# A conditional residual adapter on Trainium2: the opening puts the rows into four partition quarters with one product, shuffles 17 of them, and copies W1 later

## The chip, the cores and the metric

The kernel runs on one core of a Trainium2 chip. The metric is the device time of one execution in microseconds. Several engines work side by side, each in the order of its own queue: PE (TensorE, matrix products), DVE (VectorE), ACT (ScalarE), POOL (GpSimd), and SP (SyncE), which here only issues transfers (DMAs).

## The reference

There are 128 batches of a 128 x 512 activation. Each batch has a language id; the id selects one of ten sets of weights.

```python
w1 = W1[language_ids]                      # 512 x 128 for each batch
w2 = W2[language_ids]                      # 128 x 512
h = relu(einsum('bsh,bha->bsa', x, w1) + b1[language_ids][:, None, :])
adapted = einsum('bsa,bah->bsh', h, w2) + b2[language_ids][:, None, :]
y = x + adapted
normed = (y - mean(y)) * rsqrt(var(y) + 1e-5)          # over the 512
out = x + normed * gamma[language_ids][:, None, :] + beta[language_ids][:, None, :]
```

All data are float32. gamma, beta, b1 and b2 are drawn, so none of them can be left out.

## The kernel before

**One batch.** The 128 sequence positions lie on the partitions. PE transposes x in four 128 x 128 pieces into PSUM (`transpose_x`, L235), ACT copies them to SBUF (`copy_xT`, L239), PE makes four products with the batch's W1 (`down`, L258), ACT applies the relu with b1 as bias (`relu`, L266), and PE makes the product with W2 (`up`, L275) into one of five PSUM buffers called py. DVE adds x and sums the row (`residual`, L292), ACT squares and sums (`square`, L315), small operations make the mean and the reciprocal deviation, DVE subtracts the mean and multiplies with gamma (`scale`, L358), then multiplies with the deviation and adds (`finish`, L367). What is added there was made earlier by POOL: o = x + beta (`add_beta`, L252). b2 is added in one of three ways: by POOL as r = x + b2 (`add_b2`, L245), by DVE in PSUM (`vector_b2`, L285), or by PE as a second product into the same PSUM buffer (`b2_by_matmul`, L274). A py buffer is free again when `finish` has read it, so `up(b)` waits for `finish(b-5)`.

**The loop.** Iteration i issues on PE `transpose_x(i)`, `down(i-1)` and `up(i-2)`; the vector work of batch i-3 follows. All orders on the engines are written out by hand: `keep` chains each instruction to the one before it on its engine.

**The tables.** beta, gamma and b2 are ten rows of 512 each, and every engine needs the row of its batch on all 128 partitions. So an opening spreads all 30 rows: the rows are split into three bf16 parts (`parts`, 96 partitions), and for each row a product with a 0/1 column of `pick` puts the sum of the three parts on all 128 partitions (`spread`, L206), from where DVE or ACT copies it to its table (L211, L209). The 30 rows are interleaved with the work of the first four batches. Before that PE makes products of ones that nobody reads (`spin`, L486).

**The weights.** W2 is kept whole in SBUF. W1 comes three ways. Batches 0 to 8 load their own W1 from HBM (`load_first`, L154). From batch 9 on ACT copies it from a table in SBUF (`stage_w1`, L226): batches 9 to 20 (`EARLY = 21`) from w1e, whose rows are laid out so that the transposes of x must take every fourth column; later ones from w1, loaded in four pieces of 640 KB (`load_w1`, L103) in iterations 8, 10, 12 and 14, with transposes of adjacent columns. SP issues in this order: ids, gamma, x of batches 0-1, W2 of three languages, W1 of batches 0 and 1, x 2-3, W1 2 and 3, the rest of W2, x 4-5, W1 4 and 5, x 6-7, W1 6 and 7, x 8-9, half of w1e, W1 8, the other half of w1e, x 10-11, then x 12-15 and on in fours. The small rows of beta, b2 and b1 come by ACT's queue.

**The end.** The last five batches have an order of their own (`tail`), in which POOL takes part of the last multiplications and additions.

Of the kernel before, what the change touches and what calls it, by code (L numbers as in the profile page):

```python
# [16 lines left out]
P = 128  # L17
G = 4
EPS = 1e-5
FIRST = 9  # L20
EARLY = 21
LATE = 12
U = 2

# [2 lines left out]
def cond_resid_kernel(ctx: ExitStack, tc: tile.TileContext, x, itok, W1, b1, W2, b2, gamma, beta, out):  # L27
# [18 lines left out]
    def keep(ins):  # L46

        engine = ins.ins.engine
        if engine in last:
            tc.add_manual_dep(ins.ins, last[engine], behind, reason="kept order")  # L50
        last[engine] = ins.ins.name
        return ins
# [31 lines left out]
    x_0 = xp.tile([P, G, H], FP, tag="x", name="x_0")  # L84
    xs[0] = x_0

    def load_part(lo, hi):
        dst = xs[lo // G][:, lo % G : lo % G + hi - lo, :]
        keep(nc.sync.dma_start(out=dst, in_=x[lo:hi].rearrange("b s h -> s b h")))

    keep(nc.sync.dma_start(out=ids, in_=itok.rearrange("(o b) -> o b", o=1)))
    keep(nc.scalar.dma_start(out=rows[0:L, :], in_=beta))
# [1 line left out]
    keep(nc.scalar.dma_start(out=rows[2 * L : 3 * L, :], in_=b2))  # L94
    load_part(0, 2)
    keep(nc.scalar.dma_start(out=b1r, in_=b1))

    warm = const.tile([P, 1], FP, name="warm")
    keep(nc.vector.memset(warm, 1.0))
    keep(nc.scalar.activation(warm, warm, AF.Abs_reciprocal_sqrt))  # L100
    def load_w1(k):
        keep(
            nc.sync.dma_start(out=w1[:, :, k, :], in_=W1[:, k * P : (k + 1) * P, :].rearrange("l p a -> p l a"))  # L103
        )

    ident = const.tile([P, P], FP, name="ident")
    make_identity(nc, ident)
    eps = const.tile([P, 1], FP, name="eps")
    nc.gpsimd.memset(eps, EPS)
    ones = const.tile([P, P], BF, name="ones")  # L110
    nc.gpsimd.memset(ones, 1.0)

    R = 3 * L
    parts = const.tile([P, H], BF, name="parts")
    keep(nc.vector.memset(parts.bitcast(mybir.dt.uint32), 0))
    pick = const.tile([96, R], BF, name="pick")
    both = st.tile([P, R], FP, tag="both", name="both", bufs=1)[:96, :]
    keep(nc.vector.tensor_tensor(both, ident[:96, 0:R], ident[:96, 32 : 32 + R], ALU.add))  # L120
    keep(nc.vector.tensor_tensor(pick, both, ident[:96, 64 : 64 + R], ALU.add))
    keep(nc.vector.tensor_scalar(pick[:, L : 2 * L], pick[:, L : 2 * L], -0.5, None, ALU.mult))

    lids, w1s = {}, {}

# [25 lines left out]
    def load_first(b):  # L151
        w1s[b] = wp.tile([P, KC, A], FP, tag="w1s", name=f"w1s_{b}")
        src = W1[bass.ds(lid(b, ET.SP), 1)].rearrange("o (p k) a -> p (o k a)", k=KC)
        keep(nc.sync.dma_start(out=w1s[b].rearrange("p k a -> p (k a)"), in_=src))  # L154
# [9 lines left out]
    load_w2(0, 3)  # L164
    load_first(0)
    load_first(1)
    load_part(2, G)
    load_first(2)
    load_first(3)
    load_w2(3, L)  # L170
    xs[1] = xp.tile([P, G, H], FP, tag="x", name="x_1")
    for b in (G, G + 2):
        load_part(b, b + 2)
        load_first(b)
        load_first(b + 1)
    xs[2] = xp.tile([P, G, H], FP, tag="x", name="x_2")
    load_part(2 * G, 2 * G + 2)
    load_early(0, 5)
    load_first(2 * G)
    load_early(5, L)  # L180
    load_part(2 * G + 2, 3 * G)

    left = rp.tile([P, H], FP, tag="r", name="left")
    keep(nc.vector.tensor_copy(parts[0:R, :], rows[0:R, :]))
    keep(nc.vector.tensor_tensor(left[32 : 32 + R, :], rows[0:R, :], parts[0:R, :], ALU.subtract))
    keep(nc.vector.tensor_copy(parts[32 : 32 + R, :], left[32 : 32 + R, :]))
    keep(nc.vector.tensor_tensor(left[64 : 64 + R, :], left[32 : 32 + R, :], parts[32 : 32 + R, :], ALU.subtract))
    keep(nc.vector.tensor_copy(parts[64 : 64 + R, :], left[64 : 64 + R, :]))

    b1T = const.tile([P, L], FP, name="b1T")  # L190

# [10 lines left out]
    def spread(r, copier):  # L202
        t = (beta_b, gamma_b, b2_b)[r // L]
        row = p_y.tile([P, H], FP, tag="y", name=f"row_{r}")
        pick_r = pick[:, r : r + 1].to_broadcast([96, P])
        keep(nc.tensor.matmul(row, lhsT=pick_r, rhs=parts[:96, :], start=True, stop=True))  # L206
        dst = t[:, r % L * H : (r % L + 1) * H]
        if copier is nc.scalar:
            keep(nc.scalar.copy(dst, row))  # L209
        else:  # L210
            keep(nc.vector.tensor_copy(dst, row))  # L211

    xT, hT, rs, os, ys, ssqs, nmeans, rstds = {}, {}, {}, {}, {}, {}, {}, {}
    phs, pxs, sums = {}, {}, {}


    def b2_by_matmul(b):
        return b in (5, B - 2, B - 1)

    def b2_by_vector(b):  # L220
        return b < 4 or 8 <= b < B - 8 and (b % 4 == 1 if b < 24 else b % 16 in (1, 6, 11) or b % 32 == 30)

    def stage_w1(b):
        w1s[b] = wp.tile([P, KC, A], FP, tag="w1s", name=f"w1s_{b}")
# [43 lines left out]
    def up(b):  # L268
        v = lid(b, ET.PE)
        ys[b] = p_y.tile([P, H], FP, tag="y", name=f"py_{b}")  # L270
        m = b2_by_matmul(b)
        if m:
            pick_b = pick[:, bass.ds(v + 2 * L, 1)].to_broadcast([96, P])
            keep(nc.tensor.matmul(ys[b], lhsT=pick_b, rhs=parts[:96, :], start=True, stop=False))  # L274
        keep(nc.tensor.matmul(ys[b], lhsT=hT[b], rhs=w2[:, bass.ds(v * H, H)], start=not m, stop=True))  # L275
        del hT[b]
# [27 lines left out]
    def scalar_means(g):  # L304
        nmeans[g] = st.tile([P, 2], FP, tag="nmean", name=f"nmean_{g}")
        keep(nc.scalar.activation(nmeans[g], sums[g], AF.Copy, scale=-1.0 / H))  # L306
# [36 lines left out]
    def deviation(g):  # L343
        root(ssqs[g], of_pair(g)[0])
# [29 lines left out]
    def on(b):  # L374
        return 0 <= b < B
# [106 lines left out]
    def spin(n, width):  # L482
        idle = p_s.tile([P, H], FP, tag="s", name="idle")
        for _ in range(n):
            keep(
                nc.tensor.matmul(  # L486
                    idle[:, :width], lhsT=ones, rhs=ones[:, 0:1].to_broadcast([P, width]), start=True, stop=True
                )
            )


    spin(9, H)
    spin(1, H // 2)

    def spread_turn(lo, hi):
        for r in range(lo, hi):
            spread(r, nc.scalar if r % 7 in (1, 3, 5) else nc.vector)

    def x_turn(b):
        transpose_x(b)  # L500
        copy_xT(b)

    x_turn(0)
    transpose_b1()
    spread_turn(0, 4)
    x_turn(1)
    spread_turn(4, 11)
    down(0)
    relu(0)
    spread_turn(11, 15)  # L510
    down(1)
    relu(1)
    x_turn(2)
    spread_turn(15, 19)
    x_turn(3)
    down(2)
    relu(2)
    spread_turn(19, 24)
    down(3)
    relu(3)  # L520
    spread_turn(24, R)
    up(0)
    up(1)

    for i in range(3, B + U):
        b = i - U - 1
        if b > G and b % G == 2 and b // G + 3 < NG:
            load_x(b // G + 3)
        if i == 5:
            load_x(3)  # L530
        if i in (8, 10, 12, 14):
            load_w1((i - 8) // 2)
        if i == 4:
            up(2)
        if i == 5:
            up(3)
        if i > 3 and on(i):
            transpose_x(i)
        if b <= E:
            add_b2(b + 2)  # L540
            add_beta(b)
        if i > 4 and on(i - 1):
            down(i - 1)
        if i > 3 and on(i):
            copy_xT(i)
        if b == 2:
            scalar_means(0)
            deviation(0)
        if i > 4 and on(i - 1):
            relu(i - 1)  # L550
        if i + 1 >= LATE and on(i + 1):
            stage_w1(i + 1)
        if i > 5 and on(i - U):
            up(i - U)


        g, half = divmod(b, 2)
        p = g - 1
        mine, old = 0 <= p < B // 2, 0 <= p - 1 < B // 2
        if b == E:  # L560
            add_b2(b + 3)
            add_beta(b + 1)
            add_b2(b + 4)
            for n in range(b + 2, B):
                add_beta(n)
        if b > E:
            tail(b)
        elif half == 0:
            if on(b):
                vector_b2(b)  # L570
                residual(b)
                square(b)
            if mine:
                scale(2 * p)
                rstd(p, 1)
            if old:
                finish(2 * p - 1)
                store(p - 1)
        else:
            if on(b):  # L580
                vector_b2(b)
            if mine:
                rstd(p, 2)
            if on(b):
                residual(b)
                square(b)
            if mine:
                rstd(p, 3)
                scale(2 * p + 1)
            if mine:  # L590
                finish(2 * p)
        if 0 < g and b <= E and half == 1:
            scalar_means(g)
            deviation(g)
        if FIRST <= i + 1 < LATE:
            stage_w1(i + 1)

        for n, engine in ((i + 3, ET.Activation), (i - U + 3, ET.PE), (b + 1, ET.DVE), (b + 5, ET.Pool)):
            if on(n):
                lid(n, engine)  # L600

# [36 lines left out]
```

## Time and profile before

| what | us |
|---|---|
| median of 3 runs | 307.46 (307.35 to 307.74) |
| the profiled execution | 307.08 |
| its span, first to last instruction | 305.3 |
| PE busy | 294.6 (97%) |
| DVE busy | 295.5 (97%) |
| POOL busy | 283.7 (93%) |
| ACT busy | 282.1 (92%) |
| 128 `residual`, mean ns of one | 693 (with r), 699 (with x) |
| 126 `scale`, 122 `finish`, mean ns of one | 755, 750 |
| POOL's 128 + 96 additions, mean ns of one | 1294, 1295 |
| W2's larger load, 1792 KB, issue to landing | 10.0 |

The table's first rows are of whole executions, the rest is from the profiled one. Four engines are busy for more than nine tenths of the span, so a share of busy time does not say which of them sets the end; the chain of waits and the rows of each stage do. Instructions of one engine overlap a little, so the step from one start to the next is shorter than one duration.

### The profile page before, as it was taken

The numbers are of one execution on the slowest core, as the hardware profiler recorded it, in microseconds if no ns is written. First come the engines' busy times: TensorE is split into PE (matmuls) and PEld (weight loads), VectorE is DVE, ScalarE is ACT, GpSimd is POOL, SyncE is SP. The second block draws the span as 40 slices with busy tenths as digits, with TensorE's granted clock in tenths as the row PEclk, the third lists the DMA queues.
The fourth block names the chain that finished last, engine by engine and source line by source line (L and its number), as shares of the span: only waits on it lengthen the run. The fifth ranks groups of instructions, "written<-read, shape, count | busy, mean of one in ns | idle before, by whom it ended". The sixth has DMA issues, their size and how long they took to land.

```text
span 305.3 us, 6987 instructions
## 1 busy us (share of the span) xinstructions
PE 294.6 (97%) x1836; PEld 220.2 (72%) x1836; DVE 295.5 (97%) x770; ACT 282.1 (92%) x777; POOL 283.7 (93%) x239
## 2 busy tenths in 40 slices
PE   8999999999999999999999999999999999999980
PEld 3748787777777777777777777777777777777740
DVE  6889999999999999999999999999999999999995
ACT  3758999999999999999999999999999999999982
POOL 1349898999999999999999999999999999999995
PEclk9999999999999999999999999999999999999996
DMA  6999999966678667766877666778766767782244
GB/s 234 393 386 387 373 370 355 375 226 251 212 273 273 232 200 232 244 254 224 275 247 235 223 210 251 254 241 275 258 196 221 237 240 235 275 276 105 112 166 172
DMA packets 44057, 77.85 MB, mean 255 GB/s; under 512 B 1993, under 2 KB 7892, under 8 KB 44018
## 3 DMA queue, kind: packets, MB, share of 16 engines
q1 hardware_dynamic: 43382, 76.84, 72.8%
q10 hardware_dynamic: 636, 0.57, 0.6%
q8 instruction: 15, 0.25, 0.3%
q14 instruction: 24, 0.20, 0.2%
HBM read 43.85 MB, written 33.55 MB: 253 GB/s over the span
## 4 chain that ended last, share of the span: by engine, by line
PE 92%; DVE 5%; issue 1%; ACT 1%; DVEq 0%; POOL 0%; ACTq 0%; POOLq 0%
PE ph L258 36%; PE py L275 34%; PE pxT L235 18%; PE row L206 2%; DVE py L358 2%; PE idle L486 1%; DVE py L292 1%; DVE o L367 1%; DVE b_b L211 0%; ACT n L414 0%; ACT sq L315 0%; ACT sq L400 0%; DVE o L425 0%; ACT w1s L226 0%; DVE rstd L334 0%
## 5 line engine op out<-in xcount | busy, mean ns | idle before, releaser
L252 POOL TENSOR_TENSOR o<-x,beta_b 128x512 f32<-128x512 f32 x128 | 163.7, 1294 | 10.5 <-DVE beta_b L211 9.5
L258 PE MATMUL ph<-xT,w1s 128*128 128x128 f32 x1024 | 135.3, 275 | 0.0
L275 PE MATMUL py<-w,hT 128*128 x256 | 131.1, 595 | 0.5 <-DVE b_b L211 0.5
L245 POOL TENSOR_TENSOR r<-x,b_b 128x512 f32<-128x512 f32 x96 | 124.3, 1295 | 7.1 <-DVE b_b L211 6.2
L258 PEld LDWEIGHTS ph<-xT,w1s 128*128 128x128 f32 x1024 | 124.9, 192 | 1.0 <-ACT hT L266 0.5
L235 PEld LDWEIGHTS pxT<-ident,x 128*128 128x128 f32 x512 | 66.6, 151 | 65.3 <-issue 49.3
L358 DVE SCALAR_TENSOR_TENSOR py<-py,nmean,gamma_b 128x512 f32<-128x512 f32 x126 | 95.2, 755 | 0.2
L367 DVE SCALAR_TENSOR_TENSOR o<-py,rstd,o 128x512 f32<-128x512 f32 x122 | 91.4, 750 | 0.0
L315 ACT ACTIVATE sq<-py,sum 128x512 f32<-128x512 f32 x124 | 85.8, 692 | 2.8 <-DVE py L292 2.6
L235 PE MATMUL pxT<-ident,x 128*128 128x128 f32 x512 | 78.2, 276 | 0.0
L239 ACT COPY xT<-pxT 128x512 f32<-128x512 f32 x128 | 74.7, 583 | 3.6 <-PE pxT L235 3.6
L292 DVE SCALAR_TENSOR_TENSOR py<-py,r 128x512 f32<-128x512 f32 x96 | 66.6, 693 | 0.2
L226 ACT COPY w1s<-w 128x512 f32 x107 | 65.6, 613 | 0.0
L266 ACT ACTIVATE hT<-ph,b1T 128x128 f32<-128x128 f32 x128 | 46.9, 366 | 8.2 <-PE ph L258 2.9
L275 PEld LDWEIGHTS py<-w,hT 128*128 128x128 f32 x256 | 39.2, 192 | 2.7 <-issue 1.0
L315 ACT ACTIVATION_READ_ACCUMULATOR sq<-py,sum 128x1 f32 x124 | 25.1, 202 | 0.0
L292 DVE SCALAR_TENSOR_TENSOR py<-py,x 128x512 f32<-128x512 f32 x32 | 22.4, 699 | 0.4
L285 DVE TENSOR_TENSOR py<-py,b_b 128x512 f32<-128x512 f32 x29 | 20.2, 697 | 0.7 <-PE py L275 0.6
L325 ACT ACTIVATE root<-ssq,eps 128x2 f32<-128x2 f32 x62 | 16.4, 265 | 0.0
L292 DVE DVE_READ_ACCUMULATOR py<-py,r 128x1 f32 x96 | 13.8, 143 | 0.0
L306 ACT ACTIVATE nmean<-sum 128x2 f32<-128x2 f32 x62 | 12.3, 198 | 0.0
L329 DVE SCALAR_TENSOR_TENSOR part<-ssq,root 128x2 f32<-128x2 f32 x62 | 9.4, 152 | 0.2 <-ACT root L325 0.2
(55 smaller groups left out, 92.0 us busy)
## 6 DMA issues: line engine op xcount, KB each, us to landing
out_dram<-o SPq DMA_DIRECT2D x61, 512.0 KB, 3.4
x<-in_x_dram SPq DMA_DIRECT2D x29, 1024.0 KB, 6.6
x<-in_x_dram SPq DMA_DIRECT2D x6, 512.0 KB, 8.7
w1e<-in_L_cond_W_dram SPq DMA_DIRECT2D x2, 1280.0 KB, 12.4
w<-in_L_cond_W_dram SPq DMA_DIRECT2D x4, 640.0 KB, 8.0
w1s<-in_L_cond_W_dram SPq DMA_DIRECT2D x9, 256.0 KB, 8.1
w<-in_L_cond_W_dram SPq DMA_DIRECT2D x1, 1792.0 KB, 10.0
w<-in_L_cond_W_dram SPq DMA_DIRECT2D x1, 768.0 KB, 5.3
```

Source lines behind the costliest of these rows:

```text
L226: keep(nc.scalar.copy(w1s[b].rearrange("p k a -> p (k a)"), src))
L235: keep(nc.tensor.transpose(pxs[b][:, k, :], cols, ident))
L239: keep(nc.scalar.copy(xT[b], pxs.pop(b)))
L245: keep(nc.gpsimd.tensor_tensor(rs[b], xb(b), b2_b[:, bass.ds(v * H, H)], ALU.add))
L252: keep(nc.gpsimd.tensor_tensor(os[g][:, j, :], xb(b), beta_b[:, bass.ds(v * H, H)], ALU.add))
L258: nc.tensor.matmul(phs[b], lhsT=w1s[b][:, k, :], rhs=xT[b][:, k, :], start=(k == 0), stop=(k == KC - 1))
L266: keep(nc.scalar.activation(hT[b], phs.pop(b), AF.Relu, bias=b1T[:, bass.ds(lid(b, ET.Activation), 1)]))
L275: keep(nc.tensor.matmul(ys[b], lhsT=hT[b], rhs=w2[:, bass.ds(v * H, H)], start=not m, stop=True))
L292: nc.vector.scalar_tensor_tensor(ys[b], ys[b], 1.0, r, ALU.mult, ALU.add, accum_out=col(sums, b))
L315: nc.scalar.activation(sq, ys[b], AF.Square, bias=col(sums, b), scale=-float(H), accum_out=col(ssqs, b))
L358: nc.vector.scalar_tensor_tensor(ys[b], ys[b], col(nmeans, b), gamma_b[:, bass.ds(v * H, H)], ALU.add, ALU.mult)
L367: nc.vector.scalar_tensor_tensor(o, ys.pop(b), rstds[g][:, j : j + 1], o, ALU.mult, ALU.add)
```

## The change

The opening's rows are spread in two ways instead of one. `sel` is a matrix that repeats the 30 columns of `pick` in four quarters, so that one product (`four_copies`) puts all 30 rows, summed, on each quarter of 32 partitions; DVE copies that to SBUF, and one `stream_shuffle` per row then copies lane r of each quarter to all its 32 lanes. The ten rows of beta and the last seven of b2 are made so, on DVE. The other 13 (all of gamma and three of b2) are spread by products as before, all copied by ACT. The three parts of the rows are cut by reading the upper halves of the float32 words, two copies on ACT and two subtractions on DVE in place of three copies and two subtractions on DVE. There are 7 products of ones at the start, one more between the picks, and one and a half ahead of `up(0)`.

Batches 0 and 1 get b2 from PE, batch 5 from POOL; 2 and 3 stay with DVE. beta is added two batches earlier in POOL's order: the first four batches' as soon as the table is there, and after that the addition of beta for batch b follows that of b2 for the same b. The products of the first batches stand in another order: `up(0)`, `x_turn(4)`, `up(1)`, and `up(2)`, `up(3)` in the loop's regular places. w1e now serves batches 9 to 29 (`EARLY = 30`), and the four pieces of w1 are loaded in iterations 16, 18, 20 and 22. The order of the other loads is the same.

```diff
-EARLY = 21
+EARLY = 30
...
-    pick = const.tile([96, R], BF, name="pick")
...
+    pick = const.tile([96, 32], BF, name="pick")
...
+    sel = const.tile([96, P], BF, name="sel")
+    keep(
+        nc.vector.tensor_copy(
+            sel.rearrange("k (q r) -> k q r", q=4),
+            pick.rearrange("k (o r) -> k o r", o=1).to_broadcast([96, 4, 32]),
+        )
+    )
...
-    keep(nc.vector.tensor_copy(parts[0:R, :], rows[0:R, :]))
-    keep(nc.vector.tensor_tensor(left[32 : 32 + R, :], rows[0:R, :], parts[0:R, :], ALU.subtract))
-    keep(nc.vector.tensor_copy(parts[32 : 32 + R, :], left[32 : 32 + R, :]))
-    keep(nc.vector.tensor_tensor(left[64 : 64 + R, :], left[32 : 32 + R, :], parts[32 : 32 + R, :], ALU.subtract))
-    keep(nc.vector.tensor_copy(parts[64 : 64 + R, :], left[64 : 64 + R, :]))
+    def upper(lo):
+        return rows[lo : lo + R, :].bitcast(BF)[:, 1 : 2 * H : 2]
+    keep(nc.vector.tensor_tensor(rows[32 : 32 + R, :], rows[0:R, :], upper(0), ALU.subtract))
+    keep(nc.scalar.copy(parts[0:R, :], upper(0)))
+    keep(nc.vector.tensor_tensor(parts[64 : 64 + R, :], rows[32 : 32 + R, :], upper(32), ALU.subtract))
+    keep(nc.scalar.copy(parts[32 : 32 + R, :], upper(32)))
...
+    def four_copies():
+        t = p_y.tile([P, H], FP, tag="y", name="four_p")
+        keep(nc.tensor.matmul(t, lhsT=sel, rhs=parts[:96, :], start=True, stop=True))
+        fours[0] = rp.tile([P, H], FP, tag="r", name="four")
+        keep(nc.vector.tensor_copy(fours[0], t))
+    def shuffle_rows(lo, hi):
+        for r in range(lo, hi):
+            t = (beta_b, gamma_b, b2_b)[r // L]
+            keep(nc.vector.stream_shuffle(t[:, r % L * H : (r % L + 1) * H], fours[0], [r] * 32))
...
     def b2_by_matmul(b):
-        return b in (5, B - 2, B - 1)
+        return b in (0, 1) or b >= B - 2
     def b2_by_vector(b):
-        return b < 4 or 8 <= b < B - 8 and (b % 4 == 1 if b < 24 else b % 16 in (1, 6, 11) or b % 32 == 30)
+        return b in (2, 3, 9, 13, 17, 21) or 24 <= b < B - 8 and (b % 16 in (1, 6, 11) or b % 32 == 30)
...
-    spin(9, H)
-    spin(1, H // 2)
...
+    spin(7, H)
+    four_copies()
+    spread(10, nc.scalar)
+    spin(1, H)
     x_turn(0)
     transpose_b1()
-    spread_turn(0, 4)
+    spread(11, nc.scalar)
+    shuffle_rows(0, 10)
     x_turn(1)
...
+    add_beta(0)
+    add_beta(1)
+    spread(20, nc.scalar)
+    spread(21, nc.scalar)
     down(3)
     relu(3)
-    spread_turn(24, R)
+    spread(22, nc.scalar)
+    add_beta(2)
+    add_beta(3)
+    shuffle_rows(23, 30)
+    spin(1, H)
+    spin(1, H // 2)
     up(0)
+    x_turn(4)
     up(1)
...
-        if i in (8, 10, 12, 14):
-            load_w1((i - 8) // 2)
-        if i == 4:
-            up(2)
-        if i == 5:
-            up(3)
-        if i > 3 and on(i):
+        if i in (16, 18, 20, 22):
+            load_w1((i - 16) // 2)
+        if i > 4 and on(i):
             transpose_x(i)
         if b <= E:
             add_b2(b + 2)
-            add_beta(b)
+            if 4 <= b + 2 <= E:
+                add_beta(b + 2)
...
-        if i > 5 and on(i - U):
+        if i > 3 and on(i - U):
             up(i - U)
```

## The prediction

> **What bounds the kernel now.** I read the page first, then the chain of waits, the stages by time, and the transfers.
>
> ```profile
> span 305.3 us, 6987 instructions
> PE 92%; DVE 5%; issue 1%; ACT 1%; DVEq 0%; POOL 0%; ACTq 0%; POOLq 0%
> ```
>
> The span is followed back through PE for 92%. The early part of that chain, in order of time:
>
> ```profile
> 17.19 0.45 PE row L206 x2
> 17.64 0.02 issue
> 17.66 1.30 DVE b_b L211 x2
> 18.96 2.81 PE py L275 x6
> ```
>
> PE's only long stand is here: `up(0)` at 18.96 waited for DVE to empty a buffer. From then on PE takes 2.22 us per batch, and from batch 21 on 2.19. The cause is the transposes, whose four starts take 0.47 us with strided columns and 0.44 without:
>
> ```profile
> 56.02 0.63 PE L235 MATMUL pxT<-ident,x 128*128 128x128 f32 x4
> 56.49 1.06 PE L258 MATMUL ph<-xT,w1s 128*128 128x128 f32 x8
> ...
> 58.24 0.60 PE L235 MATMUL pxT<-ident,x 128*128 128x128 f32 x4
> 58.68 1.06 PE L258 MATMUL ph<-xT,w1s 128*128 128x128 f32 x8
> ```
>
> The stages show a second limit under the opening: the DMA engines are full from 5 us on, whatever the compute engines do (the last columns are clock, DMA share and GB/s).
>
> ```profile
> 5.00:7.50 2.50, 2.44 (x12) 1.44 (x11) 1.49 (x4) 0.85 (x2) 0.00 (x0) 1.00 1.03 387
> 17.50:20.00 2.50, 2.04 (x8) 0.85 (x7) 1.96 (x4) 1.62 (x4) 0.32 (x1) 1.00 1.06 391
> ```
>
> So the landing times of the opening's loads are given by bytes, and the order of loads stays. The second half of w1e (issued at 18.09), x 10-11 (issued at 18.77) and W2's rest (issued at 6.05), each from a DMA view of a narrow window around its issue, with the time to landing last:
>
> ```profile
> w1e<-in_L_cond_W_dram SPq DMA_DIRECT2D x1, 1280.0 KB, 13.4
> x<-in_x_dram SPq DMA_DIRECT2D x1, 512.0 KB, 14.1
> w<-in_L_cond_W_dram SPq DMA_DIRECT2D x1, 1792.0 KB, 10.0
> ```
>
> They land at 31.5, 32.87 and 16.05. Who needs them, by the timelines of ACT, PE and POOL:
>
> ```profile
> 32.21 0.60 ACT L226 COPY w1s<-w1e 128x512 f32 x1
> 33.82 0.63 PE L235 MATMUL pxT<-ident,x 128*128 128x128 f32 x4
> 32.98 1.28 POOL L245 TENSOR_TENSOR r<-x,b_b 128x512 f32<-128x512 f32 x1 [0.94 <-DMA x<-in_x_dram]
> ```
>
> The first is the copy of W1 for batch 9, the second the transposes of batch 10, the third POOL's r of batch 10, which already waits for that load and starts 0.11 after it landed. ACT has only 0.7 us in hand on w1e, PE 0.95 on x 10-11. However early the opening becomes, batch 10 cannot come earlier than these loads.
>
> **The change, part by part.** *Parts.* DVE loses three copies and keeps two subtractions (start to start 0.715 each, from 3.13): it is done at 4.56, not 5.88. ACT, free at 3.58, makes two copies of at most 0.58 (its whole-row copies): about 4.7.
>
> *PE's start.* Seven products of ones at 0.43 end near 4.0, PE stands 0.7, then the quarter product and row 10 at 0.43 each, one more of ones, transposes 0.6 to 0.85, b1's: DVE can copy b1 at 7.0 and shuffle from 7.2. The shuffle's row is not in the trace. Nearest are whole-tile DVE instructions of one pass, 0.61 from start to start; above, two passes, 1.22. I take 0.61 plus the shortest DVE step in the trace, 0.06 (the small `part` operations), for the list of lanes that differs each time: 0.67. 17 of them end at 18.6 (17.6 to 28). The Trainium skill (VectorE: DVE Perf Modes, section on the perf-mode tier table) gives about 2400 ns for a shuffle of 2048 elements; a quarter of it, 0.6, is an estimate by which the shuffles would end at 17.4.
>
> *ACT.* 13 copies at 0.54 (two take 1.07), four transposed copies at 0.5 and four relus at 0.37 are 10.5 us; from 5.7 that is 16.2, with gaps about 17. PE's own work there is 14 products of 0.22, four transposes of 0.47 and four `down` of 0.89: 8.5 us, no bound.
>
> *up(0).* W2 lands at 16.05. Batches 0 and 1 cost PE 0.22 more each; x 4-5 stands behind W2 with 512 KB at 387 GB/s, so 17.4. Then: `up(0)` 16.1, transposes of 4 at 17.4, `up(1)` 17.9, `up(2)` 18.95, transposes of 5 at 19.8, `down(4)` 20.3, `up(3)` 21.2, transposes of 6 at 22.05, `down(5)` 22.5. Before, `down(5)` started at 25.08, and batch 10's transposes 8.74 later, 0.22 of it batch 5's b2 product, now POOL's. So PE would reach batch 10 at 31.0, 2.8 earlier than before.
>
> *The load.* It cannot: x 10-11 lands at 32.87, 0.11 to wake, 0.1 for the weight load: 33.05 instead of 33.82. ACT starts batch 9's copy at 31.6, steps 0.51 and copies xT by 32.7, just inside. PE keeps **0.75** of 2.8, and stands 2 us in front of it. This stand also hides what I have not priced exactly: the opening may be up to 2 us later at no cost. For DVE, 14 us of work lie between the last shuffle and `residual(8)`, due at 35.3, with some 0.8 of waits: the shuffles may end at 20.5, so 0.78 each.
>
> *After the load.* Nine batches (21 to 29) get strided transposes, +0.03 each. Does it reach the end? DVE is nearly without idle time from 38.5 on, but at batch 26 it stands on PE (ended 75.99, next at 76.05):
>
> ```profile
> 75.24 0.75 DVE L367 SCALAR_TENSOR_TENSOR o<-py,rstd,o 128x512 f32<-128x512 f32 x1
> 76.05 0.70 DVE L292 SCALAR_TENSOR_TENSOR py<-py,r 128x512 f32<-128x512 f32 x1
> ```
>
> `up(26)` comes after the transposes of 28, eight of the nine, so 0.24 goes on to DVE: **0.75 - 0.24 = 0.51**.
>
> *POOL.* b2 of batch 5 adds 1.23 (start to start). Its additions of beta start at 13.9 and run through; at r of batch 10 it again meets 32.98, but has two additions more behind it (2.47). The next needs the first store's buffer, and that store lands behind x 12-15: 32.87 + 1.5 MB at 390 GB/s = 36.9, a wait of 2.7, against 0.94 of waits for stores and others left out. POOL ends 0.7 earlier, enough: before, its last addition ends at 302.02, DVE's at 302.08.
>
> *w1 later.* SP issues the four pieces near 47 to 60 instead of 30.6 to 45.3; 8 us to land, needed near 76: free. If that cover were gone, ACT would wait. SP's queue past them holds stores and x loads that have 5 us and more in hand. The DVE's two lost b2 additions (1.2) end in the same stand.
>
> The sum is 0.51 off the profiled 307.08 (span 305.3 and 1.8 around it), so 306.57; the median stands 0.38 above that execution: **306.95**.
>
> **The rivals.** *A: the loads land earlier, or the stand is not there.* PE then keeps 2.8 - 0.24: 304.9. For it: ACT and PE never waited for these loads before, so their landing is seen, not their need. Against: the DMA share of 1.03 to 1.06.
>
> *B: the shuffle is dear.* It decides from 0.78 each; at 0.9 it is 2.1 us, 309.0; at two passes 7.5, 314.5. For it: no row shows one. Against: every one-pass DVE row of this size.
>
> *C, slower: PE's clock falls in its 2 us stand.* In the rows, products of ones step 0.43 until 5.3 and transposes 0.21 until 6.4, later 0.117: PE works at half speed for 5.2 us after its start. At half speed for 5.2 us it loses up to 2.6: 309.5. Against: the clock column is still 1.00 in 298.0 to 299.5, after the last product at 296.4, and 0.68 in the next slice: it fell after 3.7 us without work, and 2 is less. The same holds for the 0.7 us ahead of the quarter product, whose price the stand hides. The Trainium skill (TensorE: Matmul & The Clock Gate, section on HAM oscillation) names gaps of over about 3.4 us as what slows the clock; by it C would not come, though a longer stand would, and a window of 3.4 at half speed would cost 1.7: 308.65.
>
> *D: the last additions of POOL take it back.* If the first store lands 0.5 later, POOL ends later than DVE: 307.3.
>
> **How the numbers follow.** The measurement tells about 0.2%, 0.61 us, from no change; the forecast lies just inside. Forecast 0.62: a rate of 383 to 400 GB/s over 31 us puts the landing 0.6 to either side, 306.3 to 307.5, so 0.26 of it falls beyond 306.85 and 0.36 within. A 0.12, faster. B 0.08 and C 0.08, slower. D 0.10, within. Faster 0.38, same 0.46, slower 0.16. The range reaches half into A and into the cheap ends of B and C: 306.0 to 308.2; the likeliest case alone has 306.3 to 307.5.
>
> **What would show it.** In the changed profile: no DMA slice under 1.0 before 30 us; `up(0)` at 16.1 behind W2; shuffles 0.67 apart, ending by 20.5; ACT standing before the first w1s copy until 31.6; PE standing some 2 us before transposes at 33.05, and `down(21)` to `down(29)` at 2.22. I am wrong if PE does not stand there, if its steps double after the stand, or if DVE's first residual is later than 20.9.

## The result, and the profile after

The changed kernel takes 306.73 us (median; 306.47 to 307.08) against 307.36 for the kernel before on the same chips. One of its 14 executions took 385.91 us at a mean granted clock of 0.753, for which no cause is known; the range and the ratio leave it out. The ratio is 0.9981, with a 95% interval of 0.9973 to 0.9990: 0.63 us less, on the line between "faster" and "within 0.2%". The profiled execution takes 306.72 us against 307.08, so there the gain is 0.36.

The page has the span and, from its fourth part, the shares of the chain that ended last. PE no longer carries 92% of it; POOL has 15% and the loads of the opening 8%.

```profile
span 305.0 us, 6995 instructions
PE 59%; POOL 15%; DMA 8%; issue 8%; DVE 7%; SPq 1%; ACT 1%; POOLq 0%; DVEq 0%; ACTq 0%
```

The chain in order of time (start, length, what) shows where: the opening is one transfer behind the other, and near the end it runs through POOL's additions.

```profile
7.89 10.38 DMA w1s<-in_L_cond_W_dram
18.28 13.49 DMA w1e<-in_L_cond_W_dram
...
289.96 3.70 POOL o L277 x3
```

DVE's timeline: the first and the last of the 17 shuffles.

```profile
7.52 0.75 DVE L236 STREAM_SHUFFLE beta_b<-four 128x512 f32<-128x512 f32 x1
...
17.84 0.78 DVE L236 STREAM_SHUFFLE b_b<-four 128x512 f32<-128x512 f32 x1
```

Sixteen steps in 10.32 us are 0.645 each, and the first residual, at 20.88 in the old opening, is at 18.54. PE's timeline at `up(0)` (in brackets the idle time and what ended it):

```profile
17.12 0.38 PE L299 MATMUL py<-parts,pick 96*128 96x512 bf16 x1 [0.55 <-ACT b_b L221]
```

The row names the last of ACT's 13 copies, which empties a PSUM buffer and ends at 17.13. That this copy sets the time isn't shown: in the first experiment below it ended at 16.83, `up(0)` started 1.08 later, the row names no wait (`issue`), and PE stood the same 0.55. In all twelve kernels with the new opening, PE stands 0.55 or 0.56 us between the products of ones and `up(0)`, whatever the row names; what it does there is open. `up(0)` is still 1.8 us earlier than before (18.96). Up to batch 8 PE keeps a lead of 2.04 us (its transposes start at 27.34, before at 29.38). Then come the loads. From two narrow DMA views, with the time to landing last, the second half of w1e (issued at 18.28) and x 10-11 (issued at 18.96):

```profile
w1e<-in_L_cond_W_dram SPq DMA_DIRECT2D x1, 1280.0 KB, 13.5
```
```profile
x<-in_x_dram SPq DMA_DIRECT2D x1, 512.0 KB, 14.2
```

They land at 31.8 and 33.1, a quarter of a microsecond later than before. The stages from 5 to 30 us show no room (a DMA share of 1.02 to 1.06, 382 to 393 GB/s), and now ACT, PE and POOL all stand in front of these loads:

```profile
31.85 0.62 ACT L251 COPY w1s<-w1e 128x512 f32 x1 [1.61 <-DMA w1e<-in_L_cond_W_dram]
```
```profile
33.26 0.72 PE L260 MATMUL pxT<-ident,x 128*128 128x128 f32 x4 [1.32 <-ACT hT L291]
```
```profile
33.26 1.28 POOL L270 TENSOR_TENSOR r<-x,b_b 128x512 f32<-128x512 f32 x1 [0.55 <-DMA x<-in_x_dram]
37.09 1.28 POOL L277 TENSOR_TENSOR o<-x,beta_b 128x512 f32<-128x512 f32 x1 [2.55 <-DMA out_dram<-o]
```

For PE the row names ACT's relu, the last thing that ended ahead of it, but these transposes don't read it. POOL's r of batch 10, which needs x 10-11 and nothing of ACT's, starts in the same moment, here as in the runs below (34.55 and 34.54, for instance): it is the load that both wait for. ACT's copies behind w1e end at 32.95, so w1e is a second wall 0.2 us in front of it. The lead is 0.56 at batch 10 (33.82 before), 0.47 from batch 11 on, and falls over the nine batches with strided transposes:

```profile
55.55 0.63 PE L260 MATMUL pxT<-ident,x 128*128 128x128 f32 x4
...
57.77 0.63 PE L260 MATMUL pxT<-ident,x 128*128 128x128 f32 x4
```

These are batches 20 and 21, 2.22 apart and 0.47 ahead of 56.02 and 58.24. From here on the kernel before steps by 2.19 and this one by 2.22. By batch 29 the lead is 0.24 (75.53 against 75.77), and it stays there to the end. DVE follows at batch 26: 75.81 against 76.05. At the end two engines stop close together, DVE at 301.83 (before 302.08) and POOL at 301.52 (before 302.02), by their timelines:

```profile
300.95 0.88 DVE L450 SCALAR_TENSOR_TENSOR o<-py,rstd,o 128x256 f32<-128x256 f32 x2
```
```profile
298.75 2.77 POOL L443 TENSOR_TENSOR o<-n,o 128x256 f32<-128x256 f32 x4
```

### The profile page after: what moved, and what is told of

The parts are those of the page before. It is cut to its first block, busy times and chain, and to the rows that moved or that the text cites. A ratio compares the mean times of both kernels' runs of the same rounds, so it can differ in the third digit from the quotient of the medians.

```text
span 305.0 us, 6995 instructions
## 1 busy us (share of the span) xinstructions
PE 292.6 (96%) x1821; PEld 220.0 (72%) x1821; DVE 294.4 (97%) x784; ACT 282.8 (93%) x779; POOL 285.0 (93%) x240
## 4 chain that ended last, share of the span: by engine, by line
PE 59%; POOL 15%; DMA 8%; issue 8%; DVE 7%; SPq 1%; ACT 1%; POOLq 0%; DVEq 0%; ACTq 0%
PE ph L283 24%; PE py L300 23%; PE pxT L260 12%; POOL o L277 8%; POOL r L270 6%; DMA w1e<-in_L_cond_W_dram 4%; DMA w1s<-in_L_cond_W_dram 3%; DVE py L383 2%; DVE py L317 2%; DVE o L392 1%; DVE py L310 1%; SPq L162 1%; SPq L89 0%; SPq L144 0%; ACT n L439 0%
## 5 line engine op out<-in xcount | busy, mean ns | idle before, releaser
L277 POOL TENSOR_TENSOR o<-x,beta_b 128x512 f32<-128x512 f32 x128 | 172.3, 1381 | 15.3 <-DVE beta_b L236 12.7
L270 POOL TENSOR_TENSOR r<-x,b_b 128x512 f32<-128x512 f32 x97 | 134.1, 1384 | 0.6 <-DMA x<-in_x_dram 0.6
L260 PEld LDWEIGHTS pxT<-ident,x 128*128 128x128 f32 x512 | 68.2, 155 | 66.7 <-issue 48.6
L251 ACT COPY w1s<-w 128x512 f32 x98 | 60.0, 613 | 0.0
L317 DVE SCALAR_TENSOR_TENSOR py<-py,x 128x512 f32<-128x512 f32 x31 | 21.7, 699 | 1.1 <-PE py L300 0.8
L310 DVE TENSOR_TENSOR py<-py,b_b 128x512 f32<-128x512 f32 x27 | 18.7, 691 | 0.1
L251 ACT COPY w1s<-w1e 128x512 f32 x21 | 12.8, 612 | 1.6 <-DMA w1e<-in_L_cond_W_dram 1.6
```

What stands on the lines that cost most here:

```text
L251: keep(nc.scalar.copy(w1s[b].rearrange("p k a -> p (k a)"), src))
L260: keep(nc.tensor.transpose(pxs[b][:, k, :], cols, ident))
L270: keep(nc.gpsimd.tensor_tensor(rs[b], xb(b), b2_b[:, bass.ds(v * H, H)], ALU.add))
L277: keep(nc.gpsimd.tensor_tensor(os[g][:, j, :], xb(b), beta_b[:, bass.ds(v * H, H)], ALU.add))
L317: nc.vector.scalar_tensor_tensor(ys[b], ys[b], 1.0, r, ALU.mult, ALU.add, accum_out=col(sums, b))
```

## Experiments

The theory after this reading, L: the landing of x 10-11 takes all of the opening's gain but 0.47, and the strided transposes take half of that. Two questions go beyond it. How much does POOL, which stops 0.3 us ahead of DVE, count? And would a longer stand of PE have cost its clock?

**A later opening.** Five more products of ones ahead of `up(0)`.

```diff
-    spin(1, H)
+    spin(6, H)
     spin(1, H // 2)
     up(0)
```

> The changed kernel with five more products of ones ahead of up(0), 5 x 0.216 = 1.1 us on PE. Theory L (PE stands in front of batch 10 until x 10-11 has landed, 1.3 us in the profile of the changed kernel, and whatever the opening loses before that costs nothing): the time stays within 0.2 us of the changed kernel's 306.7, and PE's stand before the transposes of batch 10 shrinks from 1.3 to about 0.2 us. Rival O (the opening's length is what was gained, so that it goes through to the end): 307.8.

Measured: 306.8 us, ratio 0.9977 (0.9967 to 0.9987). PE's timeline:

```profile
17.91 0.38 PE L299 MATMUL py<-parts,pick 96*128 96x512 bf16 x1 [0.55 <-issue]
...
33.26 0.72 PE L260 MATMUL pxT<-ident,x 128*128 128x128 f32 x4 [0.52 <-ACT hT L291]
```

`up(0)` moved from 17.12 to 17.91, the stand before batch 10 shrank from 1.32 to 0.52, and the transposes of batch 10 stayed at 33.26. The opening's length costs nothing while it lies within the stand: L holds.

**More bytes ahead of the load.** A needless 512 KB load behind x 8-9.

```diff
     load_part(8, 10)
+    keep(nc.sync.dma_start(out=w1[:, 0:2]..., in_=W1[0:2]...))
```

> The changed kernel with one needless load of 512 KB (two languages of W1, into the table that is loaded again much later) behind x 8-9, so that both halves of w1e and x 10-11 land 512 KB / 390 GB/s = 1.35 us later. Theory L: the transposes of batch 10 start at 34.6 instead of 33.26 and the end comes 1.35 later, 308.05. Rival O: the loads had time in hand, as they had before, and the time stays within 0.3 of 306.7.

Measured: 309.52 us (307.62 to 310.1), ratio 1.0050 (1.0032 to 1.0069). Batch 10 came at 34.55, as L says, but the time is 1.5 us longer than that makes it. PE's timeline and two stages of this kernel (the last columns are clock, DMA share and GB/s):

```profile
34.55 0.72 PE L261 MATMUL pxT<-ident,x 128*128 128x128 f32 x4 [2.75 <-ACT hT L292]
```
```profile
32.00:34.50 2.50, 0.00 (x0) 0.00 (x0) 2.01 (x5) 1.35 (x4) 0.00 (x0) 1.00 1.05 388
35.30:38.70 3.40, 3.40 (x12) 2.26 (x11) 0.06 (x1) 2.73 (x8) 0.84 (x2) 0.50 1.05 405
```

POOL's r of batch 10 starts at 34.54. PE stood 2.75 us at full clock, started again, and 0.8 us later ran at half clock for 3.4 us; from 38.8 on the clock is 1.00 again. The twelve executions fall in two groups: four of 307.62 to 308.25 with a mean clock of 0.990 to 0.994, eight of 309.43 to 310.1 with 0.983 to 0.984. 3.4 us at half speed are 1.7, the distance of the groups.

**The same bytes, PE kept busy.** Eleven products of ones ahead of batch 10's transposes, at first into the PSUM buffer of those transposes.

```diff
         pxs[b] = p_x.tile([P, KC, P], FP, tag="xT", name=f"pxT_{b}")
+        if b == 10:
+            for _ in range(11):
+                keep(nc.tensor.matmul(<pxs[10]>, lhsT=ones, rhs=<ones>, start=True, stop=True))
```

> The kernel with 512 KB of needless loads, in which PE stood 2.75 us in front of batch 10 and then worked at half clock for 3.4 us, with eleven products of ones (2.4 us) in that stand that nobody reads. Theory, the stand lets the clock fall, which costs 1.7 us: PE's steps keep their full rate behind the stand, no run lies near 309.5, and all are near 307.8 (308.3 at most). Rival, the lower clock has another cause, or the later load alone costs the 2 us: the median stays at 309.5.

Measured: 311.54 us (309.96 to 311.91), ratio 1.0117 (1.0097 to 1.0137): a miss, by the edit itself. There is one buffer for transposes, and ACT empties it of batch 9 only behind the copy that waits for w1e. PE's timeline:

```profile
34.54 4.22 PE L259 MATMUL pxT<-ones 128*128 128x512 bf16 x11 [2.52 <-ACT xT L273]
```

PE stood 2.52 us all the same, the clock fell once more (0.59 in 35.3 to 38.7), and the products came behind the stand, nearly all at half speed, so that batch 10 began at 38.60. By the mean clocks this happened in three of the five executions: two are at 309.96 and 309.98 with a mean clock of 0.990 and 0.991, the three others at 311.54 to 311.91 with 0.985 to 0.987. The second attempt writes them to the PSUM buffer of batch 8's result, which is free at 31.8:

```diff
...
+        if i == 10:
+            ys[8] = p_y.tile([P, H], FP, tag="y", name="py_8")
+            for _ in range(11):
+                keep(nc.tensor.matmul(ys[8], lhsT=ones, rhs=<ones>, start=True, stop=True))
         if i > 4 and on(i):
             transpose_x(i)
```

> The kernel with 512 KB of needless loads again, in which PE stood 2.75 us and the clock then fell, now with eleven products of ones in the PSUM buffer of batch 8's result, which is free at 31.8 us (in the run before this they had to wait for a buffer until 34.5, and so came behind the stand). Theory, a stand that fills most of a window of 3.41 us lets the clock fall: the products keep PE busy from 31.8 to 34.2, batch 10's transposes come at 34.55 as without them, the granted clock stays full, and all runs lie at 307.6 to 308.3 with a mean clock of 0.99. Rival, the later load alone costs it: median 309.5.

Measured: 308.03 us (307.72 to 308.84, all at a clock of 0.989 to 0.994), ratio 1.0021 (1.0012 to 1.0030). PE's timeline and the stage that had the low clock:

```profile
31.85 2.55 PE L577 MATMUL py<-ones 128*128 128x512 bf16 x11
34.45 0.72 PE L261 MATMUL pxT<-ident,x 128*128 128x128 f32 x4
```
```profile
35.30:38.70 3.40, 3.40 (x23) 2.69 (x23) 1.66 (x5) 3.40 (x11) 0.83 (x2) 1.00 1.05 406
```

Useless work in the stand takes 1.5 us off the median, which is now that of the faster group. So the clock is shown as the cause of the slower group, and what is left, 1.3 us above the changed kernel, is the landing alone: batch 10 starts 1.19 later.

**The loads moved ahead.** x 10-13 ahead of w1e; batches 9 to 11 with their own W1.

```diff
-FIRST = 9
+FIRST = 12
...
     load_part(8, 10)
-    load_early(0, 5)
     load_first(8)
-    load_early(5, L)
     load_part(10, 12)
+    load_first(9)
+    load_part(12, 14)
+    load_first(10)
+    load_early(0, 5)
+    load_first(11)
+    load_early(5, L)
+    load_part(14, 16)
...
-        if i == 5:
-            load_x(3)
```

> The changed kernel with the late loads in another order: batches 9, 10 and 11 also load their own W1, x 10-11 and x 12-13 come ahead of w1e, and w1e is needed from batch 12 on only. It costs 768 KB more of transfers. Theory L alone: PE keeps the 2.0 us by which it is ahead at batch 8, less 0.24 for the strided transposes: 305.2. Theory L with POOL (POOL's additions of beta have to wait for the first store's buffer, which lands behind all these loads, now at about 39.2 instead of 37.0, and POOL has no time in hand after that): POOL becomes the bound, its whole order moves by 2.1 us and the time is about 308.7.

Measured: 309.2 us (308.44 to 310.25), ratio 1.0057 (1.0037 to 1.0077). PE started batch 10 at 31.61, 2.2 ahead: these loads were the wall. But the first store now queues behind more bytes, and POOL, whose buffers of o it frees, stood:

```profile
40.06 1.27 POOL L283 TENSOR_TENSOR o<-x,beta_b 128x512 f32<-128x512 f32 x1 [6.09 <-DMA out_dram<-o]
```

POOL ended at 304.3. Two more kernels take that back in part. First, beta two batches later again:

```diff
-            if 4 <= b + 2 <= E:
-                add_beta(b + 2)
+            if b >= 4:
+                add_beta(b)
```

> The loads moved ahead as in the run before (x 10-11 and x 12-13 ahead of w1e, batches 9 to 11 with their own W1), and beta in the order of the kernel before: the addition of beta for batch b follows that of b2 for batch b+2. Theory, POOL and its wait for the first store set the end of that run: POOL now makes two more additions of b2 (2 x 1.233 us) ahead of the addition that waits for the first store, so its end comes 2.5 us earlier, and POOL alone would give about 306.8 us; PE's lead of 2.2 less 0.24 would give 305.2. The later of the two counts: 306.8. Rival, the moved loads themselves cost something on PE or ACT: about 309.2 again. Rival, only the order counted and POOL's amount of work does not: 305.2.

Measured: 307.9 us (307.83 to 308.04), ratio 1.0017 (1.0004 to 1.0029), between the cases. POOL's end came 1.5 earlier, not 2.5, since POOL went on behind the first store only at 40.56; and w1e landed at 38.0, where ACT stood 2.04, so that PE's lead was down to 0.22 at batch 29. The expectation had left out that w1e becomes the next wall (in the run before this, too, ACT stood 1.74 for it). Second, with b2 of batches 4 to 6 by PE as well:

```diff
-        return b in (0, 1) or b >= B - 2
+        return b in (0, 1, 4, 5, 6) or b >= B - 2
```

> The same with b2 of batches 4, 5 and 6 by PE: three products of 0.22 us more on PE, three additions of 1.233 us less on POOL. Theory, POOL sets the end where PE's lead is kept: POOL alone would now give 303.2 us, PE alone 2.2 - 0.24 - 0.66 = 1.3 us less than the kernel before, 306.0; so 306.0, less than the kernel without this edit although PE has more work. Rival, PE or the loads set the end: 0.66 us more than the kernel without this edit.

Measured: 307.89 us (307.0 to 308.9), ratio 1.0017 (1.0000 to 1.0033); expected were 306.0. The profiled execution is the fastest of the six, 307.0 us; why the others take up to 1.9 longer is open. Even it is 1.0 above the expectation, and shows why. PE was 1.05 ahead of the kernel before at batch 29 (74.72 against 75.77) and still at batch 118 (270.13 against 271.18); DVE ended at 301.02, POOL at 302.01 (in the kernel before 302.02). POOL's three spared additions lie ahead of its wait for the first store and became waiting (5.2 us instead of 3.9 for that store, and 2.8 instead of none for x). In this execution a full microsecond of PE's is worth nothing, because POOL ends as before.

**POOL in the changed kernel.** b2 of batches 4 to 6 by PE, loads as they are (the last diff alone).

> The changed kernel with b2 of batches 4, 5 and 6 by PE and its loads as they are. PE's 0.66 us more lie in front of the load of x 10-11, in the stand of 1.3 us, and cost nothing; POOL has 3.7 us less to do. Theory, the landing of that load and PE's rate behind it set the end, POOL just follows: 306.7 us, within 0.2 of the changed kernel. Rival, POOL still sets the end of the changed kernel: up to 0.4 us less, 306.3. Rival, PE's stand was no room at all: 307.4.

Measured: 306.64 us, ratio 0.9977 (0.9964 to 0.9990): no change against the changed kernel. PE's 0.66 were hidden in the stand. POOL's 3.7 turned into waiting here too (5.24 for x 10-11, 2.64 for the store), so this run says nothing on POOL's end. An addition more behind the last wait does:

```diff
-            keep(nc.gpsimd.tensor_tensor(rs[b], xb(b), b2_b[...], ALU.add))
+            for _ in range(2 if b == 40 else 1):
+                keep(nc.gpsimd.tensor_tensor(rs[b], xb(b), b2_b[...], ALU.add))
```

> The changed kernel, in which POOL makes the addition of b2 for batch 40 twice (the same values again): 1.233 us more on POOL behind its last wait, nothing more elsewhere. Theory, POOL has no more than 0.3 us in hand at the end: 307.6 to 307.9 us. Rival, POOL has the 2.2 us in hand that its additions of b2 show against DVE: 306.7.

Measured: 307.7 us (307.21 to 307.87), 0.97 more than the changed kernel for 1.233 of work. So POOL has little in hand: 0.26 us by this difference, 0.31 by its end in the profile of the changed kernel. Both are estimates: the interval of this run's time is 0.28 to either side, and POOL's end moved by 1.66 between the two profiled executions (from 301.52 to 303.18), more than the added work.

**Which part moved POOL's end?** The order of beta undone in the changed kernel (the same diff as in the first run above with beta two batches later, but the loads as they are):

> The changed kernel with beta in the order of the kernel before: the addition for batch b behind that of b2 for batch b+2. PE and DVE have the same work at the same places. Theory, the end hangs on POOL as much as on PE, and the earlier beta is what moved POOL's end forward: POOL now makes r of 10, 11 and 12 and beta of 8 and 9 between 33.26 and 39.4 us and starts beta of 10 there, 0.3 later than the kernel before (39.17), so its end falls back to that kernel's or behind it, 307.4 us. Rival, PE's lead of 0.24 and DVE behind it set the end: 306.7.

Measured: 306.69 us (306.37 to 306.9), ratio 0.9976 (0.9967 to 0.9985): no change, so not this part. POOL then waits 2.67 for x 10-11 and not at all for stores. W1's part undone:

```diff
-EARLY = 30
+EARLY = 21
...
-        if i in (16, 18, 20, 22):
-            load_w1((i - 16) // 2)
+        if i in (8, 10, 12, 14):
+            load_w1((i - 8) // 2)
```

> The changed kernel with the W1 part undone: w1e serves batches 9 to 20 only and the four pieces of w1 are loaded in iterations 8 to 14 as before. PE alone: nine batches get 0.03 us back, 0.24 by batch 26, so 306.45. With POOL (the pieces stand ahead of the second to fourth stores, whose buffers POOL waits for; about 0.8 and 1.0 us more of waits at the additions of beta of batches 12 and 16): POOL sets the end and the time is about 308.2.

Measured: 308.33 us (308.05 to 308.69), ratio 1.0022 (1.0006 to 1.0039), though PE is 0.5 ahead at batch 100 (231.09 against 231.61). POOL's timeline has three waits for stores, two of them new:

```profile
37.13 1.28 POOL L277 TENSOR_TENSOR o<-x,beta_b 128x512 f32<-128x512 f32 x1 [2.64 <-DMA out_dram<-o]
43.25 2.51 POOL L277 TENSOR_TENSOR o<-x,beta_b 128x512 f32<-128x512 f32 x2 [1.14 <-DMA out_dram<-o]
53.04 1.28 POOL L277 TENSOR_TENSOR o<-x,beta_b 128x512 f32<-128x512 f32 x1 [1.09 <-DMA out_dram<-o]
```

The trace holds the landing of only three or four of the seven stores issued between 20 and 60 us. The one issued near 38 took 8.4 us to land here, 7.6 in the kernel before and 4.2 in the changed one; the one near 56 took 6.1, 4.9 and 5.6. The four 640 KB pieces of W1 are issued at 47 to 61 us in the changed kernel and at 31 to 45 in the kernel before, where they meet the loads of x. There the DMA engines are full from 33 to 48 us (a share of 1.07 to 1.09); in the changed kernel the share is down to 0.13 from 45 to 48. Last, the kernel before without b2 of batch 12:

```diff
-        if not b2_by_matmul(b) and not b2_by_vector(b):
+        if b != 12 and not b2_by_matmul(b) and not b2_by_vector(b):
```

> The kernel before without b2 of batch 12, which POOL adds there behind its wait for x 10-11: DVE adds x alone, PE and DVE keep their work, POOL has 1.233 us less. Theory, POOL sets the tail of the kernel before (its product with gamma starts as soon as its last additions of beta end, at 295.3): 306.9 to 307.1 us. Rival, PE and DVE set it: 307.35, no change.

Measured: 307.24 us (307.03 to 307.5), ratio 0.9999 (0.9990 to 1.0008): no change, but not for the rival's reason. POOL waited 2.0 for stores instead of 0.8 (at 43.25 and 52.72; before, at 52.53 only), so nearly all of the 1.233 spared was spent there, and in the profiled execution POOL ended last, at 302.2 against DVE's 301.64. Whether POOL sets the end of the kernel before is not told by this run.

No version beats the changed kernel by more than 0.1 us, which these intervals don't resolve.

## Why the prediction was right, point by point

- **Parts and shuffles.** 4.7, 0.67 each and 18.6 forecast; 4.73, 0.645 and 18.62 measured. That the end agrees so closely is luck: the shuffles began 0.3 later than forecast (7.52 instead of 7.2) and each is a little shorter, between the 0.67 and the 0.6 that the prediction works out. Rival B, a dear shuffle, is out.
- **`up(0)`.** 16.1 forecast, 17.12 measured. The step took W2's landing as the only condition. It left out the 0.55 us that PE stands behind the products of ones, and ACT's last copy, which it had itself put at "about 17"; both fit 17.12, and the runs don't tell them apart in this kernel. It cost nothing and shortened the stand from 2 to 1.32 us.
- **The load.** Mis-sized by 0.26: x 10-11 landed at 33.13 instead of 32.87, batch 10 came at 33.26 instead of 33.05. PE kept 0.56, and 0.47 from batch 11 on, not 0.75. That the landing of these loads sets batch 10 is shown from both sides, by the later opening (no cost) and by the bytes (1.19 later, 1.3 longer). The bytes delayed w1e as well; that x 10-11 is the later of the two, by 0.2, is read from the rows alone. Rival A is out.
- **After the load.** 0.24 forecast, 0.23 measured (0.47 to 0.24). DVE's end moved by 0.25: the sum was 0.25, not **0.51**, and the difference comes from the load.
- **From the profile to the median.** The forecast added 0.38 because the median before lay so far above its profiled execution. The changed kernel's median is its profiled time. The sum of 306.57 lay 0.15 below the profiled 306.72, the offset of 0.38 was 0.37 too much, and the forecast of 306.95 lay only 0.22 above the median because the two errors cancel in part. That is luck. Of the gain of 0.36 between the profiled executions, 0.11 is not traced: DVE's end moved by 0.25. Why the old kernel's executions lie above its profiled one is open; that its POOL and DVE stop within 0.06 us of each other, and that its stores land late, would fit, but was only argued.
- **POOL.** First store 36.9 and wait 2.7 forecast; POOL went on behind it at 37.09 after a wait of 2.55. End 0.7 earlier forecast, 0.5 measured. Rival D did not come, by some 0.3 us. The step with the largest error is **w1 later**, priced as free. It costs nothing, but only its own landing was weighed; what it leaves behind, faster stores while POOL's buffers depend on them, is worth 1.6 us in this kernel (308.33 against 306.73, the 0.24 that it costs PE already taken off), and without it the change would have been slower. POOL's sum counted the wait for the first store alone; that the later ones are gone is this step's doing, and the prediction doesn't say so.
- **PE's clock.** Rival C did not come, and its place was judged rightly, but not its bound. The reason given against it was that the clock fell after 3.7 us without work at the end and 2 is less; stands of 2.52 and 2.75 us sufficed, in some executions. A stand of 2 us, as forecast, was not measured. The price given for a window at half speed, 1.7, was right.

The Trainium skill (TensorE: Matmul & The Clock Gate, section on HAM oscillation) names gaps of over about 3.4 us; by the measured stands that is too long, and the measurement decides. The Trainium skill (the same page, section on what is actually happening) says that the window of 3413 ns is free-running. The traces agree: between two changes the recorded clock stays for whole multiples of it (30.72 us, or 9, before it fell in the first run with more bytes; 290.13, or 85, in the changed kernel). Counted in steps of 3.41 us from these changes, the window at whose end the clock fell held 2.65 and 2.52 us without PE's work in the two runs that show it; in the changed kernel the stand gives its window 1.22. So how a stand lies in the windows may decide, which would put one kernel's executions in two groups; no run here moves a stand on purpose to show it.

## What to carry to other kernels

An opening that is shortened in front of transfers at full rate gains only up to the next landing; read who would wait there first, and price the gain from the landing, not from the work removed. Ask of every moved load what it leaves behind as well as when it arrives: here the stores beside it, and through them an engine with some 0.3 us in hand, decided the sign. Work spared ahead of a wait becomes waiting, so spare it behind the engine's last wait, and keep a stand of PE well below the length after which its clock was seen to fall.

## What was not expected of the hardware

- The clock fell after stands of 2.52 and 2.75 us, 0.1 and 0.8 us after PE had begun again, for 3.4 us. By the times and mean clocks it did so in three of five and in eight of twelve executions; after 1.32 us it did not, nor after 1.50 in the run with W1's part undone.
- A shuffle of 128x512 f32 steps in 0.645 us, the load of its lane list included (a row of its own of 0.00 to 0.05 us).
- A 512 KB store issued near 38 us took 4.2 us to land instead of 7.6 when the 2.5 MB of W1 were loaded 16 us later.
- By the clock records of the traces, the clock became full at 9.27 us in the changed kernel and at 4.11 in the run with b2 of batches 4 to 6 by PE and the loads as they are. Batch 10 began at 33.26 and 33.19: the stand hides this too.
